# One bank per PSUM pool, the ring of exponentials turned by three places, and layer 1's first channels normalised right behind the last exponential

## The chip, the cores and the metric

The kernel runs on one core of a Trainium2 chip. The core has a matrix engine (TensorE, "PE" in the profile; its weight loads are listed as "PEld"), a vector engine (VectorE, "DVE"), an activation engine (ScalarE, "ACT"), a general engine (GpSimd, "POOL") and a queue engine (SyncE, "SP") that issues most of the transfers. Each engine works through its own queue in order and waits on semaphores for the others. Matmuls write to PSUM, which has eight banks. The metric is the device time of one execution in microseconds (us); a kernel is run several times and the median is compared.

## The reference

Two layers work on x of shape (2, 256, 64, 64): two samples of 256 channels. Cut to what matters:

```python
def _L0_conv_ref(x, qkv_w, qkv_b, num_heads):            # 8 heads of 32 channels, n = 4096 pixels
    ...
    attn_logits = jnp.einsum('bhci,bhcj->bhij', q, k) * scale
    attn_weights = jax.nn.softmax(attn_logits, axis=-1)
    out = jnp.einsum('bhij,bhcj->bhci', attn_weights, v)
...
ctx = _sa(blockify(fq), blockify(fk), blockify(v), oh, ow)   # 64 groups of 64 pixels, stride 8
feats = _bn_relu(_c1x1(ctx, lr_W_w), lr_W_scale, lr_W_shift)
...
ctx2 = _sa(qx, kx, vx, DH, DW)                               # the same on 8 x 8 neighbourhoods
...
return rate1 * out_att + rate2 * out_conv                    # out_conv: a 3 x 3 convolution
...
x = x + _L0_conv_ref(_gn(x), L0_conv_qkv_w, L0_conv_qkv_b, 8)
x = x + _L1_conv_ref(_gn(x), ...)
```

`_gn` is a group normalisation over 8 channels and all pixels. Layer 1 therefore cannot be normalised before layer 0 has ended for those channels.

## The kernel before

Everything runs sample by sample (`b` = 0, 1) through four stages, each with its own PSUM pools, opened and closed in the loop at L1497: `project0` (pool ps0: eight buffers of one bank), `attention0` (pool sc), `layer1_first` (pool ps1: eight buffers), and `layer1_second` (pool pacc with four banks for the convolution, ps2 with four buffers). `bank` takes a buffer of the current pool. A tile of a new pool waits until what lay at its address in the old pool has been read for the last time; with a pool of several banks this holds for the pool's tiles together.

**Channels.** 256 channels are two chunks of 128 (`KC` = 2, k = 0 and 1). The pixels are eight tiles of 512 (`NT`, `T`). A tile of x is `xts[t]`.

**attention0.** A head's 4096 queries are two groups of 2048, so there are 16 groups g per sample. For each group the keys come in 32 blocks j of 128 (`NJ`). A unit is one block by one quarter (512 queries): one score matmul into a bank of `ring` (seven banks of PSUM), and one exponential by ACT (L551) into a place in SBUF. The places form a ring of 28 (`RING`): places 0 to 16 are in the tile `es` (pool apool, tag A), 17 to 27 in `held["es"]`. `at_places` and `runs_of` turn a running count into a place, and split a run of two or three units where the bank ring or one of the two memories ends. `steps` lists the work behind the scores: for each block `add_rows` (DVE adds the exponentials into `added[g]`, L597; for the blocks in `SUMMED` transfers add them in memory, issued by POOL at L605 and L607) and `quarters` (PE multiplies them with the values into `av`, L560; the row sums also go through L560, with `ones`, into a bank of the ring). The loop at L821 interleaves `scores` and `steps`; the queues of PE, ACT and DVE keep the order of the program text (`manual_schedule`).

**The end of attention.** For the last group, blocks 29 to 31 (`SUMMED_LAST`) are not added by DVE: `sum_rows` lets PE sum their rows, with the memory sums `acc` and the DVE sums `added`, in two halves of 256 queries. `steps` emits these row sums behind block 28, then the av products of blocks 29 to 31. `finish_last` then computes the standard deviation of chunk 0 (Sqrt on ACT, L666; reciprocal and shift on DVE), the reciprocals of the row sums (L674), the last context y (in b = 0 copied from PSUM by ACT first, L679), y's statistics, and returns `put`, which writes y into x, and `check`. `Stats.tile` (L321) is a bn_stats per tile of x; those of chunk 1 hang on blocks of the last group.

**layer1_first.** `xg` is the normalised x, regrouped so that each of eight slices of groups takes pixels from all eight tiles t. It has apool's tag A, as `es` has, and apool has one buffer. `to_groups` writes one tile of one chunk of it, on ACT, POOL or DVE (L1171, L1174). Then come, on PE: in b = 0 `fold_products` (weights w3 and fv multiplied with lr and srw, L253 to L280), the mean and variance matmuls of chunk 1 (L328, L337), `firsts` (six projections that need chunk 0 alone), the same with chunk 1 (L1194), and `at_grid` (L1208). After that `group_attention` runs over eight slices. Its last matmuls `pc` go through `to_feats` into `feats`, and `layer1_second` starts from these (`branch`, L1367), with the image copies xp of x on ACT (L1313). In b = 0 DVE also builds the convolution's weights there (`conv_weights`, L857 to L937), whose inputs POOL loads.

**Sample 1's projections.** `following` normalises it while sample 0 ends; `heads4` (L410) projects it.

The lines that set the order at the seam:

```python
if (g, j) == (last, NJ - 3):
    assert len(places) == n_units
    held["rows"] = spare_bank()
    for i in (NJ - 3, NJ - 2, NJ - 1):
        add_rows(g, i)
    sum_rows(g, held["rows"])
```

Of the kernel before, what the change touches and what calls it, by code (L numbers as in the profile page):

```python
# [9 lines left out]
F32 = mybir.dt.float32  # L10
# [30 lines left out]
def direct_layers(ctx: ExitStack, tc: tile.TileContext, a: dict, out: bass.AP, bad: bass.AP):  # L41
# [20 lines left out]
    def bank(shape, name):  # L62
        return psum["ps"].tile(shape, F32, tag="bank", name=name)
# [132 lines left out]
    def fold_scores():  # L196
# [32 lines left out]
        for k in range(KC):  # L229
            block = slice(k * P, (k + 1) * P)  # L230
            pg = bank([P, C + AT], f"pt_g_{k}")
# [17 lines left out]
    def fold_products():  # L249
# [3 lines left out]
        for name, behind in (("w3", "lr"), ("fv", "srw")):  # L253
            turned = w4([P, KC, C], "turned_" + name)
            for j in range(KC):
                pt = bank([P, C], f"pt_{name}_{j}")
                for k in range(KC):
                    nc.tensor.transpose(pt[:, k * P : (k + 1) * P], wts[name][:, k, j * P : (j + 1) * P], ident)
                nc.scalar.copy(turned[:, j, :], pt)
            yield  # L260
            for k in range(KC):
                pt = bank([P, C], f"pm_{name}_{k}")
                for j in range(KC):
                    nc.tensor.matmul(
                        pt, turned[:, j, k * P : (k + 1) * P], outer[behind][:, j, :], start=j == 0, stop=j == KC - 1
                    )
                nc.scalar.copy(wts[name][:, k, :], pt)
            nc.sync.dma_start(out=kept_w[name], in_=wts[name])
            yield
# [138 lines left out]
    def project0(b, xn, w0):  # L408

        def heads4(nm, g):  # L410
            for t in range(NT):
                nt = f"{nm}_{b}_{g}_{t}"
                n = slice(t * T, (t + 1) * T)
                pq = bank([P, T], f"p_{nt}")
# [56 lines left out]
    SUMMED_LAST = (NJ - 3, NJ - 2, NJ - 1)  # L471

    def attention0(b, xts, held):
# [18 lines left out]
        def at_places(first, n):  # L492

            while n > 0:
                at = first % RING
# [7 lines left out]
        recent, spare = [], [0]  # L503
        ring = psum["sc"].tile([P, BANKS, T], F32, tag="ring", name=f"ring_{b}")
# [22 lines left out]
        def runs_of(n):  # L527

            at = n_places
            while n > 0:  # L530
                e = at % RING
# [43 lines left out]
        def add_rows(g, j):  # L575
            if j == 0:
                sums[g] = psum["sc"].tile([P, T], F32, tag="av", name=f"av_{b}_{g}")
# [31 lines left out]
        def work_of(g, j):  # L609


            if (g, j) < (last, NJ - 3):
# [8 lines left out]
        def sum_rows(g, rows):  # L621
            if g == last:
                for part in range(2):
                    for j in SUMMED_LAST:
                        quarters(rows, ones, lambda u: unit(g, j, u), j == SUMMED_LAST[0], False, part)
                    quarters(rows, ones, lambda u: acc[u], False, False, part)
                    quarters(rows, ones, lambda u: added[g][u // 2][:, u % 2, :], False, True, part)
# [31 lines left out]

        def finish_last(g):  # L660
# [5 lines left out]
            nc.scalar.activation(st.rstd[:, first_chunk], st.d[:, first_chunk], AF.Sqrt, bias=eps)  # L666
            rows, avs = held["rows"], copied[g]
            nc.vector.reciprocal(st.rstd[:, first_chunk], st.rstd[:, first_chunk])
            shift = small.tile([P, KC], F32, tag="gn_shift", name=f"shift_{b}")
            st.shift = shift  # L670
            shift_of(st, 0)
            for part in range(2):
                n = slice(part * T // 2, (part + 1) * T // 2)
                nc.vector.reciprocal(avs[:, 1, n], rows[:, n])  # L674
            kept = w4([P, T], f"kept_{b}")
            y = avs[:, 0, :]
            if b == 0:

                nc.scalar.copy(y, sums[g])  # L679
                nc.scalar.copy(kept, rows)  # L680
                nc.vector.tensor_mul(y, y, avs[:, 1, :])
            else:
                nc.scalar.copy(kept, rows)
                nc.vector.tensor_mul(y, sums[g], avs[:, 1, :])
# [69 lines left out]
        for t in range(NT):  # L754
            if t < NT // 2:
                at_block(last, 27 + t, lambda t=t: st.tile(1, t))
            else:
# [16 lines left out]
        def steps():  # L774

            for done in range(NH0 * 2 * NJ):
                g, j = divmod(done, NJ)
                if (g, j) == (last, NJ - 3):
                    assert len(places) == n_units
                    held["rows"] = spare_bank()  # L780
                    for i in (NJ - 3, NJ - 2, NJ - 1):
                        add_rows(g, i)
                    sum_rows(g, held["rows"])
                for _ in work_of(g, j):
# [16 lines left out]
                if j == NJ - 1:  # L801
                    waiting.append(g)
                    avs = w4([P, 2, T], f"avs_{b}_{g}")
                    if g < last:
                        nc.scalar.copy(avs[:, 0, :], sums[g])
                    copied[g] = avs
                    late[:] = [finish(g)]
                    next(late[0])
# [5 lines left out]
        with tc.manual_schedule(engines={E.PE, E.Activation, E.DVE}):  # L814
# [6 lines left out]
            while begun < NH0 * 2 * NJ:  # L821
# [13 lines left out]
                while begun < ready:  # L835
# [7 lines left out]
                    if not final and begun == NH0 * 2 * NJ - 3:  # L843
# [10 lines left out]
            return *finish_last(last), st  # L854
# [194 lines left out]
    def group_attention(nm, q, k, tokens, wv, out, busy=False, apart=False, more=None, split=False, fill=None):  # L1049
# [89 lines left out]
        for m in range(KC):  # L1139
            pc = bank([P, T], f"pc_{nm}_{m}")  # L1140
# [19 lines left out]
    def layer1_first(b, xts, put, check, st):  # L1160


        mean, rstd, shift = st.mean, st.rstd, st.shift

        xg = apool.tile([P, KC, 64, 8, 8], F32, tag="A", name=f"xg_{b}")

        def to_groups(k, t, eng):
            dst = xg[:, k, :, t, :].rearrange("p (d e) o -> p d e o", d=8)
            src = xts[t][:, k, :].rearrange("p (d o e) -> p d e o", d=8, o=8)
            if eng is nc.scalar:  # L1170
                return nc.scalar.activation(  # L1171
# [911 lines left out]
```

## Time and profile before

| | us |
|---|---|
| three runs | 3043.44, 3048.76, 3051.78 |
| median | 3048.76 |
| profiled execution, its own time | 3049.64 |
| its span | 3047.8 |
| attention of sample 0, first to last exponential | 115.13 to 1127.37 |
| attention of sample 1 | 1628.42 to 2643.48 |
| at_grid (L1208) starts | 1159.27 and 2670.63 |
| group attention over slices ends, `branch` starts | 1249.42 and 2756.41 |

Read it so: the "span" is from the first to the last record; what lies around it is 1.8 us. Busy time of PE is modelled, so a busy PE need not be at its peak. A row of a timeline or of a group has the line, the engine, what is written and from what, and in brackets how long the engine was idle before and which instruction ended that. Idle time of an engine costs only where somebody waits for that engine.

### The profile page before, as it was taken

How to read it: one execution, taken by the hardware profiler on the slowest of the kernel's cores; microseconds unless marked ns; L12 is line 12 of the kernel's file. 1: busy time of each engine (PE TensorE's matmuls, PEld its weight loads, DVE VectorE, ACT ScalarE, POOL GpSimd, SP SyncE). 2: the span in 40 equal slices, each digit the busy share in tenths (PEclk: the TensorE clock that was granted, in tenths of full speed). 3: DMA queues.
4: the chain of work that ended last, by engine and by line, in shares of the span. 5: the costliest groups of instructions: out<-in, count | busy, mean ns of one | idle time of the engine just before them, and what ended most of it. 6: DMA issues, size and time to landing. Idle time of an engine off the chain costs nothing. (4 is left out here: it accounts for less than half of the span.)

```text
span 3047.8 us, 63942 instructions
## 1 busy us (share of the span) xinstructions
PE 2972.1 (98%) x25129; PEld 1856.3 (61%) x25129; DVE 2452.3 (80%) x3120; ACT 2341.8 (77%) x3268; POOL 832.3 (27%) x918
## 2 busy tenths in 40 slices
PE   7999999999999999999999999999999999999998
PEld 4556556665556656577765555566555565576765
DVE  4598998989899999856647989989989899835543
ACT  2699999999999984632237999999999999834333
POOL 1022222322223230055401222222222222306440
PEclk9999999999999999999999999999999999999999
DMA  7978789787897761231159688797788976700000
GB/s 260 276 136 181 147 163 174 155 178 150 175 180 157 152 130 37 75 126 42 49 207 270 128 178 161 158 182 146 169 166 166 182 161 130 170 5 4 21 15 23
DMA packets 244420, 425.53 MB, mean 140 GB/s; under 512 B 98904, under 2 KB 109964, under 8 KB 241932
## 3 DMA queue, kind: packets, MB, share of 16 engines
q0 software_dynamic: 94720, 237.57, 40.4%
q1 hardware_dynamic: 149244, 183.51, 21.7%
q8 instruction: 199, 3.26, 0.4%
q14 instruction: 113, 0.93, 0.1%
q10 hardware_dynamic: 144, 0.26, 0.0%
HBM read 120.08 MB, written 68.39 MB: 62 GB/s over the span
## 5 line engine op out<-in xcount | busy, mean ns | idle before, releaser
L551 ACT ACTIVATE es<-ring 128x512 f32<-128x512 f32 (+2 forms) x1572 | 1203.5, 904 | 30.4 <-PE ring L545 22.3
L545 PE MATMUL ring<-q,k 128*128 128x512 f32 x4096 | 1081.8, 407 | 11.6 <-ACT v L551 5.5
L597 DVE TENSOR_TENSOR e<-e,es 128x1024 f32<-128x1024 f32 (+1 forms) x956 | 1035.0, 1143 | 23.3 <-ACT es L551 22.9
L545 PEld LDWEIGHTS ring<-q,k 128*128 128x128 f32 x4096 | 732.3, 188 | 382.5 <-ACT es L551 118.4
L551 ACT ACTIVATE v<-ring 128x512 f32<-128x512 f32 (+2 forms) x1024 | 780.8, 900 | 24.2 <-PE ring L545 12.5
L560 PE MATMUL av<-es,v 128*32 128x256 f32 (+1 forms) x9684 | 724.5, 389 | 0.0
L597 DVE TENSOR_TENSOR e<-e,v 128x1024 f32<-128x1024 f32 (+1 forms) x636 | 669.2, 1107 | 22.6 <-ACT v L551 21.8
L560 PE MATMUL av<-v 128*32 128x256 f32 (+1 forms) x6188 | 497.8, 388 | 0.0
L560 PEld LDWEIGHTS av<-es,v 128*32 128x32 f32 x9684 | 328.0, 109 | 264.6 <-issue 105.0
L560 PEld LDWEIGHTS av<-v 128*32 128x32 f32 x6188 | 221.1, 109 | 170.5 <-issue 72.1
L996 PE MATMUL mm<-v,wf 128*128 128x256 f32 x1024 | 227.6, 380 | 1.5 <-DVE z L1007 1.5
L607 POOL DMA_DIRECT2D es<-es x118 | 100.7, 853 | 463.6 <-ACT es L551 414.0
L996 PEld LDWEIGHTS mm<-v,wf 128*128 128x128 f32 x1024 | 193.3, 190 | 36.8 <-issue 9.8
L986 POOL TENSOR_TENSOR v<-col 128x512 f32<-128x512 f32 x128 | 165.5, 1319 | 178.0 <-ACT rk_sr L1155 39.5
L1003 ACT COPY z<-mm 128x512 f32<-128x512 f32 x32 | 18.7, 586 | 183.3 <-PE mm L996 183.3
L605 POOL DMA_DIRECT2D es<-es x20 | 11.4, 569 | 504.3 <-ACT es L551 445.1
L607 POOL DMA_DIRECT2D acc<-es x118 | 117.9, 1006 | 106.0 <-ACT es L551 40.3
L607 POOL DMA_DIRECT2D es<-v x72 | 61.3, 852 | 290.8 <-ACT v L551 287.4
L1004 DVE TENSOR_TENSOR z<-z,mm 128x512 f32<-128x512 f32 x32 | 22.0, 687 | 126.9 <-ACT z L1003 126.4
L607 POOL DMA_DIRECT2D v<-es x112 | 115.0, 1027 | 18.4 <-ACT es L551 9.0
L607 POOL DMA_DIRECT2D acc<-v x78 | 75.0, 961 | 77.7 <-ACT es L551 27.5
L982 POOL TENSOR_TENSOR col<-xp 128x1152 f32<-128x1152 f32 x32 | 69.6, 2175 | 66.6 <-DVE xp L1448 55.3
(255 smaller groups left out, 2653.0 us busy)
## 6 DMA issues: line engine op xcount, KB each, us to landing
acc<-es POOLq DMA_DIRECT2D x128, 512.0 KB, 6.4
acc<-v POOLq DMA_DIRECT2D x84, 512.0 KB, 6.4
es<-es POOLq DMA_DIRECT2D x138, 256.0 KB, 4.2
v<-es POOLq DMA_DIRECT2D x132, 256.0 KB, 5.0
k<-wk_halves SPq DMA_DIRECT2D x64, 512.0 KB
q<-wq_halves SPq DMA_DIRECT2D x256, 128.0 KB
v<-v POOLq DMA_DIRECT2D x90, 256.0 KB, 4.9
es<-v POOLq DMA_DIRECT2D x84, 256.0 KB, 3.9
```

Of the source, the lines that this page charges most:

```text
L545: touch(nc.tensor.matmul(sc[:, i, :], held["k", g // 2][:, j * P : (j + 1) * P], held["q", g, u // 2][:, u % 2, :], start=True, stop=True, ...
L551: nc.scalar.activation(dst, sc, AF.Exp, scale=SC0), set(range(at % BANKS, at % BANKS + m))
L560: note(nc.tensor.matmul(dst[HD0 * u : HD0 * u + HD0, n], lhs, rhs(u)[:, n], start=start, stop=stop))
L597: nc.vector.tensor_add(dst[:, s, :], dst[:, s, :], src)
L605: nc.gpsimd.dma_start(out=dst, in_=src)
L607: nc.gpsimd.dma_start(out=dst, in_=src, accum_op=ALU.add)
L982: (nc.gpsimd.tensor_add if plus else nc.gpsimd.tensor_sub)(col, cols(one), cols(two))
L986: (nc.gpsimd.tensor_add if plus else nc.gpsimd.tensor_sub)(dst, rows(one), rows(two))
L996: nc.tensor.matmul(mm[:, m, r, :], wf[:, k, 4 * r + q, m * P : (m + 1) * P], v[r // 2][:, r % 2, k, :], start=k == 0, stop=k == KC - 1,)
L1003: nc.scalar.copy(z[:, 1], mm[:, :, 1, :])
L1004: nc.vector.tensor_add(z[:, 0], z[:, 1], mm[:, :, 0, :])
```

## The change

**Banks.** Each stage's general pool becomes pools of one bank each (`open_banks`); `bank` goes round them by a counter, or takes a named one (`at`). The av sums get a pool of their own. The last projection of sample 1 and fold_scores' second product are put in bank 7, the last slice's pc in banks 2 and 3, and ps2 has banks 4 to 7.

**The ring.** Places are turned by three (`RING_SHIFT`). `xg` is no tile of its own but a view of `es` (`Groups`): chunk 0 is places 0 to 7, chunk 1 places 8 to 15.

**The end.** `SUMMED_LAST` has four blocks. Before the row sums, `before_last_rows` emits the Sqrt, two of chunk 1's bn_stats, the standard deviation, and chunk 0's tiles 5 to 7 on POOL and 0 and 1 on ACT; behind them `behind_last_rows` emits the reciprocals and copies by halves (two banks), ACT's tiles 2 to 4 and two more bn_stats. y is always multiplied out of PSUM. ACT's normalise runs through the elements in another order.

**layer1_first.** POOL's order is now also that of the text. `put` comes first; the fold's steps or three projections stand before chunk 1's mean matmul, one more before the variance. Chunk 1 is normalised by half tiles (four of the eight slices at a time). `fold_products` does both transposes first and yields after each product.

The diff, cut:

```diff
+    def open_banks(name, first):
+        stack = ExitStack()
+        places = range(first, 8)
+        psum.update(
+            turn=0, first=first,
+            banks={i: stack.enter_context(tc.tile_pool(name=f"{name}_{i}", bufs=1, space=PSUM)) for i in places},
+        )
+        return stack
+
+    def bank(shape, name, at=None):
+        if at is None:
+            at = psum["first"] + psum["turn"] % len(psum["banks"])
+            psum["turn"] += 1
+        return psum["banks"][at].tile(shape, F32, tag="bank", name=name)
...
+                final = b > 0 and (nm, g, t) == ("wq0", KC - 1, NT - 1)
+                pq = bank([P, T], f"p_{nt}", at=7 if final else None)
...
-    SUMMED_LAST = (NJ - 3, NJ - 2, NJ - 1)
+    SUMMED_LAST = tuple(range(NJ - 4, NJ))
+    N_LAST = len(SUMMED_LAST)
+    N_POOL = 3
+
+    RING_SHIFT = 3
...
-                at = first % RING
+                at = (first + RING_SHIFT) % RING
...
-                sums[g] = psum["sc"].tile([P, T], F32, tag="av", name=f"av_{b}_{g}")
+                sums[g] = psum["av"].tile([P, T], F32, tag="av", name=f"av_{b}_{g}")
...
+        def before_last_rows():
+
+            nc.scalar.activation(st.rstd[:, first_chunk], st.d[:, first_chunk], AF.Sqrt, bias=eps)
+            for t in range(2):
+                st.tile(1, t)
+            nc.vector.reciprocal(st.rstd[:, first_chunk], st.rstd[:, first_chunk])
+            st.shift = small.tile([P, KC], F32, tag="gn_shift", name=f"shift_{b}")
+            shift_of(st, 0)
+            held["groups"] = Groups(es, xts, st)
+            for t in range(NT - N_POOL, NT):
+                held["groups"].normalise(0, t, nc.gpsimd)
+            held["by_act"] = iter(range(NT - N_POOL))
+            by_act(2)
...
+        def behind_last_rows(g):
+
+            avs = copied[g] = w4([P, 2, T], f"avs_{b}_{g}")
+            kept = held["kept"] = w4([P, T], f"kept_{b}")
+            held["y"] = avs[:, 0, :]
+            for part, at in enumerate(held["rows"]):
+                n = slice(part * T // 2, (part + 1) * T // 2)
+                for made in (nc.vector.reciprocal(avs[:, 1, n], ring[:, at, n]), nc.scalar.copy(kept[:, n], ring[:, at, n])):
+                    for other in rows_made[1 - part]:
+                        tc.declare_no_dep(made.ins, other.ins, reason="another bank of the ring")
+                by_act(1 + part)
+            for t in range(2, NT // 2):
+                st.tile(1, t)
...
-                if (g, j) == (last, NJ - 3):
+                if (g, j) == (last, NJ - N_LAST):
                     assert len(places) == n_units
-                    held["rows"] = spare_bank()
-                    for i in (NJ - 3, NJ - 2, NJ - 1):
+                    before_last_rows()
+                    held["rows"] = []
+                    for _ in range(2):
+                        spare_bank()
+                        held["rows"].append(spare[0])
+                    for i in SUMMED_LAST:
                         add_rows(g, i)
                     sum_rows(g, held["rows"])
+                    behind_last_rows(g)
...
-                    if not final and begun == NH0 * 2 * NJ - 3:
+                    if not final and begun == NH0 * 2 * NJ - N_LAST:
                         break
...
+    class Groups:
+
+        def __init__(self, place, xts, st):
+            self.xts, self.st = xts, st
+            self.xg = place[:, 0 : KC * NT, :].rearrange("p a n -> p (a n)").rearrange(
+                "p (k g t o) -> p k g t o", k=KC, g=64, t=8
+            )
+
+        def normalise(self, k, t, eng, half=None):
+            st = self.st
+            first, n = (0, 8) if half is None else (4 * half, 4)
+            order = "p d o e" if eng is nc.scalar else "p d e o"
...
-        with tc.manual_schedule(engines={E.PE, E.Activation, E.DVE}):
+        with tc.manual_schedule(engines={E.PE, E.Activation, E.DVE, E.Pool}):
...
+            for half in range(2):
+                put(nc.gpsimd.tensor_copy, (2 * half, 2 * half + 1))
+            firsts = [lambda t=t, m=m: project(t, m, slice(0, 1)) for t in range(3) for m in range(KC)]
+            for n in range(4 if b == 0 else 3):
+                firsts.pop(0)() if b else next(fold)
+            st.means(second, bank([P, 1], f"pm_l1_{b}"), nc.vector.tensor_copy)
             st.spread(second)
+            firsts.pop(0)() if b else next(fold)
+            st.variances(second, pv := bank([P, 1], f"pv_l1_{b}"))
             st.deviations(second, pv)
             shift_of(st, 1)
...
-            for t in range(NT):
-                done = to_groups(1, t, nc.scalar if t < n_act else nc.vector)
+            for half in range(2):
+                for t in range(NT):
+                    done = groups.normalise(1, t, nc.scalar if t < n_act else nc.vector, half)
...
+                        ends=(2, 3) if t == NT - 1 else None,
```

## The prediction

> **What bounds the kernel now.** I read the engine shares first, then busy time by stretch, then the timeline at each place where one stage hands over to the next, because the title names hand-overs. The profiled execution took 3049.64 us, of which the span is 3047.8.
>
> ```profile
> PE 2972.1 (98%) x25129; PEld 1856.3 (61%) x25129; DVE 2452.3 (80%) x3120; ACT 2341.8 (77%) x3268; POOL 832.3 (27%) x918
> ```
>
> TensorE (PE) is recorded busy for all but 76 us. So a change that takes no matmul away can only win where PE is idle or slow. The chain of waits covers the last 285 us alone (nearly all PE), so I looked for idle PE by stretch. In attention (130 to 1100 us) PE is busy 967.00 of 970.00 and ACT 940.39: two engines near their limit, nothing to win. The second sample's seam between layer 0 and layer 1 looks different (columns: stretch, length, PE, PEld, DVE, ACT, POOL, granted PE clock, DMA):
>
> ```profile
> 2645.00:2650.00 5.00, 4.73 (x88) 2.60 (x80) 4.13 (x7) 0.09 (x1) 0.00 (x0) 1.00 0.08 18
> 2650.00:2655.00 5.00, 1.52 (x20) 0.36 (x8) 4.79 (x6) 4.24 (x5) 4.21 (x2) 0.91 0.58 211
> 2655.00:2660.00 5.00, 1.58 (x4) 1.01 (x5) 2.09 (x9) 2.35 (x2) 4.88 (x4) 0.50 1.02 413
> 2660.00:2665.00 5.00, 5.00 (x10) 2.33 (x9) 3.16 (x7) 3.21 (x4) 1.48 (x3) 0.56 0.76 309
> ```
>
> ACT and POOL have nothing to do from 2645 to 2650; then PE has nothing to do for two stretches, and starts again at half clock. The timeline says who waits for whom (start, duration, in brackets idle before and releaser):
>
> ```profile
> 2641.55 1.93 ACT L551 ACTIVATE v<-ring 128x512 f32<-128x512 f32 x2
> ...
> 2643.53 1.07 PE L560 MATMUL ring<-es,ones 128*32 128x256 f32 x16 [0.16 <-ACT v L551]
> ...
> 2650.79 8.14 POOL L1174 TENSOR_SCALAR xg<-x,mean_l,rstd_l 128x512 f32<-128x512 f32 x3 [11.54 <-PE av L560]
> ...
> 2655.66 0.37 DVE L325 BATCH_NORM_AGGREGATE mv_l<-stats_l 128x2 f32<-128x48 f32 x1
> ...
> 2658.98 2.07 PE L1194 MATMUL py<-xg,wt_g 128*128 128x512 f32 x2 [2.24 <-POOL xg L1174]
> ...
> 2660.84 0.42 PE L337 MATMUL pv_l<-d_l,group 128*128 128x1 f32 x2
> ```
>
> Last exponential at 2643.48; the normalised copy xg takes the exponentials' memory, so POOL starts when PE's last av matmul (to 2651.5) has released it; its third tile ends at 2658.93; the first projection starts there. Twenty py records run until at_grid (L1208) at 2670.63. The first sample is alike: POOL starts at 1134.88 [11.74 <-PE av], projections at 1148.82, at_grid at 1159.27, with weight products between. Three smaller seams each hold a PE wait:
>
> ```profile
> 1543.50 12.71 PE L416 MATMUL p_wk<-xn,wqk 128*128 128x512 f32 x29 [0.87 <-ACT res_sr L1155]
> ```
>
> ```profile
> 1627.89 2.35 PE L545 MATMUL ring<-q,k 128*128 128x512 f32 x9 [1.56 <-DVE hl_wq L422]
> ```
>
> ```profile
> 2756.41 5.40 PE L1367 MATMUL phq_sr<-feats,wt_fq 128*128 128x512 f32 x8 [2.76 <-ACT feats L1155]
> ```
>
> In none is the releaser's data needed by that first matmul: it only empties a bank of the pool before.
>
> **Main seam, second sample.** With the ring turned by three, walking the loop puts the last four blocks (16 units) in places 8 to 23, and blocks 26 and 27 in 0 to 7. So chunk 0 of xg (places 0 to 7) may be written once block 27 is consumed: PE by about 2642.4, DVE's add by 2643.23, the memory adds issued at 2638.07 plus the 6.4 us landing row by 2645.7.
>
> ACT: table load and Sqrt end at 2645.1 as now. DVE then makes rstd and shift at once (0.15 + 0.16), since block 28's two adds (2.33) are gone from its queue: 2645.5. POOL's three tiles follow: 8.14 by the row, to 2653.7. ACT does tiles 0 and 1, a half kept copy, tile 2, the other half, tiles 3 and 4: five at 1.31 less some overlap, plus 2 x 0.35, to 2652.5. Chunk 0 is complete 5.3 earlier than now.
>
> PE: only half a block of av work (0.47) remains behind the last scores, so it waits about 1.1 for the last exponential where it waits 0.16 now. Row sums: eight records take 0.44; six sets (four blocks, acc, added) in two halves make 12 x 0.44 = 5.3, to 2648.8 (now 10 sets, with a wait for DVE's block-28 add inside). Four av blocks of 0.93: to 2652.5, against 2651.5. Queued behind the row sums are av and then everything; this 1.0 is the added cost. The two reciprocals (1.7 each) and two bn_stats end on DVE by 2651.8, so y starts at 2652.6, as now (2652.46), and its chain to the aggregate takes the 3.57 of now: 2656.2.
>
> PE starts projections at 2653.7 after an idle of 1.2. Three at 0.86 (two records of 0.43): 2656.3; the mean matmul; DVE's mean and spread take 1.9 as now: 2658.4; one projection meanwhile; variance to 2658.9; 0.8 to the first chunk-1 normalise. By half tiles the first half takes ACT 3 x 0.7, DVE 5 x 0.43: ready at 2661.9, where full tiles take 3.7. The two other projections end at 2660.6, so PE waits 1.3: **this chain is what is late next.** Eight records of 0.43: at_grid at 2665.4 instead of 2670.6. **-5.2.** Put's copies (2.61 on POOL) end near 2656.7, before their readers.
>
> Here the Trainium skill's page "TensorE: Matmul & The Clock Gate" (Part 1: The HAM clock gate) matters: an idle window of about 3.4 us halves the clock, and as long a busy one restores it. The rows above agree for a 7 us gap (0.50, projections at 0.86 a record). For gaps of 1.0 to 1.3 the nearest row is the first sample's seam, where gaps of up to 2.5 go with clocks of 0.80 to 0.88. By that row 11 us at 0.8 cost 2.2 (gain 3.0), by the rule nothing (gain 5.2). I take the rule: PE is busy for only 59 to 77% of those stretches, and would be for over 80%.
>
> **Main seam, first sample.** The same sums from the last exponential at 1127.37: av ends 1136.5, chunk 0 at 1137.5, transposes and turned copies to 1138.6, w3's products to 1139.7, mean 1140.2, one fv product, variance 1142.5, the rest of the fold (1.9) to 1144.4, six projections (5.2), eight records (3.4): at_grid at 1153.0 instead of 1159.3, **-6.3**. But the convolution-weight work on DVE (L888 onwards, now from 1153.47) starts near 1149.9, only 3.6 earlier: the half tiles cost it 12 x 0.43 against 6 x 0.72. At the stage's end PE already waits behind it (bd, 1.64 and 2.34, DVE held 5.19 for weights). That stall may grow by 0 to 2.7; I take +1.4. **-4.9.**
>
> **Single banks.** Second sample's projections start when pc_sr has ended: -0.9, PE being full behind it. Its scores start as the last projection ends; ACT's own last bias copy ends at 1627.05 and the first exponential now starts at 1628.42: **-1.3**, ACT setting the ramp. In the first sample the exponential waits for its table load anyway (ends 1115.11): 0. At phq, PE gains 1.7, but hq waits for six image copies on ACT up to 2760.48 and runs now at 2761.04: **-0.5**; first sample likewise 0.3. Were ACT ordered otherwise, up to 1.7 and 1.3.
>
> **Turned places.** Splits at a place's or bank's edge: walking the loop gives 1305 exponentials per sample against 1298 (2596 on the page is twice that) and 6 more memory adds. A split costs 2 x 0.65 - 1.09, less 0.09 of overlap, 0.12: 14 make 1.7 if ACT is the limit, 0 if PE is. I take **+0.8**.
>
> **Sum:** -5.2 - 4.9 - 0.9 - 1.3 - 0.8 + 0.8 = -12.3, so 3049.6 - 12.3 = **3037.3**. The median of the runs shown, 3048.76, is 0.9 lower, inside their spread of 8, so I do not shift it.
>
> **Rivals.** (a) *New waits take half back*: clock at 0.8 in the second seam (+2.2), the whole conv-weight stall (+1.3), a pool still released as one because ring is one tile, so the three bank gains fail (+3.0): 3044. For: the rows at 0.80 to 0.88; against: busier seams. (b) *The small ends all fall well*: no stall growth (-1.4), no split cost (-0.8), ACT's image copies behind hq (-2.2): 3033. (c) *Slower*: the split that fell at place 17 (bank 3) now falls at place 0 (bank 4) once each turn of 28 places, 147 turns in all. ACT's waits for ring in attention average 0.34 (14.7 us, 43 times); a new one of 0.2 per turn costs 29: 3067. It decides from 0.09 per turn. Against: the number of edges per turn is unchanged. (d) *It does not do what it says*: were es ordered as a whole, the row sums would wait for POOL's tile at 2653.7, some +10 per sample, 20 in all, against gains of 11.5 there and 2.2 at the three smaller seams after the split cost: 3056. Against: exponentials are written into es all through attention while PE reads it, without such waits.
>
> **Chances.** Forecast 0.60 (3033 to 3041), (a) 0.13, (b) 0.20, (c) 0.05, (d) 0.02. Range 3029 to 3045: (a) and (b) with some 3 us of scatter between medians beside (b). Below about 0.3% (9.1 us) a difference cannot be told from none here: faster needs under 3039.6, which holds for (b), nine tenths of the forecast (0.55) and a little of (a) (0.02): 0.77. Slower needs over 3057.9: (c), 0.05. Same: 0.18.
>
> **What would show it.** Right: POOL's xg starts within 3 us of the last exponential and carries no wait for av; PE's gap before the first py under 2 us at clock 1.0; at_grid about 22 us after the last exponential in the second sample (now 27.1) and 25.6 in the first (now 31.9); p_wk, ring and phq without the waits above. Wrong: row sums waiting for ACT or POOL, py records of 0.86, a longer attention stage, or more PE idle before the first convolution.

## The result and the profile after

| | before | changed |
|---|---|---|
| median of 6 runs, us | 3050.27 | 3027.77 |
| lowest and highest | 3043.44, 3052.64 | 3024.22, 3033.0 |
| profiled execution, its own time | 3049.64 | 3024.22 |
| its span | 3047.8 | 3022.4 |

The ratio is 0.9932, with a 95% interval of 0.9921 to 0.9944: 22.5 us less between the medians, 25.4 between the two profiled spans. The forecast was 3037.3, 12.3 us less. The direction is right, the gain was almost double, and the measured median lies 1.2 us below the low end of the range.

The engine shares of the changed kernel first: PE is recorded busy for 9 us less than before, although it has 32 more records.

```profile
PE 2963.0 (98%) x25161; PEld 1850.1 (61%) x25161; DVE 2443.4 (81%) x3111; ACT 2341.5 (77%) x3288; POOL 843.3 (28%) x930
```

The same work takes PE less time where the granted clock is higher. Before, the profile holds nine half-clock windows of 3.4 us between 15 and 3005 us; after, two. The first sample's twenty projections show it, before (one window at their start) and after (none):

```profile
1148.82 10.52 PE L1194 MATMUL py<-xg,wt_g 128*128 128x512 f32 x20 [1.64 <-ACT xg L1171]
```

```profile
1139.60 8.83 PE L1243 MATMUL py<-es,wt_g 128*128 128x512 f32 x20
```

In the same way w3's eight products take 1.99 us where they took 3.34, and the second sample's py records 2.1 us less. Some 5 of the 12.8 us that the two hand-overs gain are such clock time.

The hand-over of the second sample by stretches of 5 us, from just after its last exponential at 2624.83 (columns: stretch, length, PE, PEld, DVE, ACT, POOL, granted clock, DMA share, GB/s):

```profile
2625.00:2630.00 5.00, 5.00 (x96) 3.02 (x98) 2.20 (x4) 4.29 (x6) 3.18 (x2) 1.00 0.02 5
2630.00:2635.00 5.00, 3.80 (x65) 1.81 (x55) 4.08 (x5) 3.76 (x4) 4.67 (x2) 1.00 0.32 105
2635.00:2640.00 5.00, 4.90 (x14) 2.12 (x15) 3.38 (x12) 0.26 (x1) 2.45 (x4) 1.00 0.93 337
2640.00:2645.00 5.00, 3.81 (x10) 1.50 (x9) 4.97 (x13) 4.72 (x8) 0.00 (x0) 1.00 1.02 417
```

ACT and POOL work at once, PE is busy for 76% of a stretch at the least, and the clock stays at 1.00. The timeline of the changed kernel at the places that the prediction named (start, duration, in brackets idle before and releaser), PE and POOL together:

```profile
2624.89 1.27 PE L582 MATMUL ring<-es,ones 128*32 128x256 f32 x17 [1.02 <-ACT v L573]
...
2626.82 7.85 POOL L1218 TENSOR_SCALAR es<-x,mean_l,rstd_l 128x512 f32<-128x512 f32 x3 [7.23 <-DVE rstd_l L688]
...
2634.92 2.81 PE L1243 MATMUL py<-es,wt_g 128*128 128x512 f32 x6 [1.20 <-POOL es L1218]
...
2642.51 3.67 PE L1243 MATMUL py<-es,wt_g 128*128 128x512 f32 x8 [1.19 <-DVE es L1218]
```

POOL starts 2.0 us after the last exponential and waits for DVE's rstd, no longer for the last output product. The two waits that are left are those the prediction worked out: 1.2 ahead of the first projection, 1.3 ahead of the first of chunk 1.

Where the 25.4 us between the two profiles went, stage by stage:

| stretch | before | after | difference | forecast |
|---|---|---|---|---|
| start to the table load ahead of the first exponential | 113.83 | 112.10 | -1.7 | 0 |
| attention 0, from that load to the last exponential | 1013.55 | 1011.23 | -2.3 | +0.4 |
| hand-over 0: last exponential to at_grid | 31.89 | 25.03 | -6.9 | -6.3 |
| layer-1 slices 0: at_grid to branch | 90.16 | 87.02 | -3.1 | +1.4 |
| branch of sample 0 to first exponential of sample 1 | 378.99 | 372.79 | -6.2 | -2.5 |
| attention 1, first to last exponential | 1015.06 | 1016.66 | +1.6 | +0.4 |
| hand-over 1 | 27.15 | 21.28 | -5.9 | -5.2 |
| layer-1 slices 1 | 85.78 | 84.10 | -1.7 | -0.5, with the next row |
| branch of sample 1 to the end | 291.44 | 292.21 | +0.8 | |

The hand-overs came out within 0.7 us of the forecast. What was not forecast lies elsewhere: attention 0, the slices, and the long stretch between the samples. Not all of these differences belong to the change. The -1.7 at the start is within the scatter: one version of the kernel (image copies on DVE, below) reaches this point at 112.25 us in one profile and at 113.57 in another. And attention 0 of the changed kernel takes 1012.5 us in its second profile (below), 1.1 less than before and not 2.3.

### The profile page after: what moved, and what is told of

Its sections match the earlier page's. It is cut to its first block, busy times and chain, and to the rows that moved or that the text cites. A ratio compares the mean times of both kernels' runs of the same rounds, so it can differ in the third digit from the quotient of the medians.

```text
span 3022.4 us, 64069 instructions
## 1 busy us (share of the span) xinstructions
PE 2963.0 (98%) x25161; PEld 1850.1 (61%) x25161; DVE 2443.4 (81%) x3111; ACT 2341.5 (77%) x3288; POOL 843.3 (28%) x930
## 3 DMA queue, kind: packets, MB, share of 16 engines
q8 instruction: 199, 3.26, 0.5%
## 4 chain that ended last, share of the span: by engine, by line
PE 87%; DVE 5%; DMA 3%; ACT 2%; issue 1%; SPq 0%; ACTq 0%; DVEq 0%; POOLq 0%
PE ring L567 32%; PE av L582 29%; PE mm L1036 7%; PE p_wk L433 2%; PE pv L456 2%; PE p_wq L433 2%; DVE prep L957 2%; PE prq_sr L1417 2%; PE prk_sr L1417 2%; PE pvs_sr L1106 2%; PE phk_sr L1406 1%; PE phq_sr L1406 1%; PE ring L582 1%; PE pvs_lr L1106 1%; PE py L1243 1%
## 5 line engine op out<-in xcount | busy, mean ns | idle before, releaser
L582 PE MATMUL av<-v 128*32 128x256 f32 x6224 | 506.0, 389 | 0.0
L629 POOL DMA_DIRECT2D acc<-es x126 | 129.5, 1033 | 116.4 <-ACT es L573 32.1
L629 POOL DMA_DIRECT2D acc<-v x86 | 87.5, 1017 | 81.9 <-DMA acc<-es 35.5
```

What stands on the lines that cost most here:

```text
L582: note(nc.tensor.matmul(dst[HD0 * u : HD0 * u + HD0, n], lhs, rhs(u)[:, n], start=start, stop=stop))
L629: nc.gpsimd.dma_start(out=dst, in_=src, accum_op=ALU.add)
```

## The experiments

My theory after the result: the hand-over gives 11 to 13 us, single banks 3 to 6, fewer clock windows the rest. Rivals: R1, the banks give much more; R2, the turned ring changes the attention itself; R3, the part not forecast is chance. (The expectations call a sample a batch.)

**Banks alone**, with the named banks and the av sums' own pool (the diff to the kernel before, cut):

```diff
+    def open_banks(name, first):
...
+    def bank(shape, name, at=None):
...
-        with tc.tile_pool(name=f"ps0_{b}", bufs=8, space=PSUM) as psum["ps"]:
+        with open_banks(f"ps0_{b}", 0):
```

> The kernel before with only the single-bank pools, the named banks and the separate pool of the output sums. My theory: they free the first tiles of a stage from waiting for the release of all eight banks of the stage before, and let the bank that is free first be taken; they are worth 3 to 6 us of the 22.5 (3044 to 3047 us, ratio 0.9980 to 0.9990), seen as the missing 0.23-us waits in the second stage and no p_wk and ring waits at the start of batch 1; the stretch from the last exponential to at_grid stays within 1 us of 31.9 and 27.15 us. Rival R1 (the pools carry most of what was not forecast): below 3040 us, ratio below 0.9965. Rival R3 (what was not forecast is chance in the clock and elsewhere): 3049 us or more, ratio 0.9995 or more.

Measured: 3042.71 us (3038.68 to 3046.35), ratio 0.9980 [0.9972, 0.9987]: 6.1 us, at the top of my own bracket. The hand-overs take 30.1 and 27.0 us (31.9 and 27.15 before). The gain sits between the samples, where the stretch from the last convolution of sample 0 to the first exponential of sample 1 falls from 101.53 to 97.24 us. PE's timeline of this run shows how, and it is not what I had forecast:

```profile
1528.48 1.02 PE L429 MATMUL p_wk<-xn,wqk 128*128 128x512 f32 x2
1529.44 1.15 PE L1103 MATMUL sp_sr<-rk_sr,rq_sr 128*64 128x64 f32 x32
1530.52 2.86 PE L1079 MATMUL pvs_sr<-wt_fv,feats 128*128 128x256 f32 x12
1533.21 1.88 PE L429 MATMUL p_wk<-xn,wqk 128*128 128x512 f32 x4
1534.93 0.38 PE L1135 MATMUL at_sr<-ident,e_sr 128*128 128x128 f32 x2
1535.15 1.03 PE L1079 MATMUL pvs_sr<-wt_fv,feats 128*128 128x256 f32 x4
1536.01 1.02 PE L429 MATMUL p_wk<-xn,wqk 128*128 128x512 f32 x2
1536.87 1.95 PE L1155 MATMUL pc_sr<-bd,vs_sr 128*128 128x128 f32 x16
```

Projections of the next sample (p_wk) stand between the small products of the last slice. With a pool of eight banks they could only follow all of it. PE's waits before, 0.45 at sp, 0.17 and 0.87 around pc, 1.56 at the first scores, are all gone. In the same way the next slice's phq now stands between the two parts of pc, where PE waited 0.23 for vs in most slices. The kernel before has the wait, and phq behind it:

```profile
2791.32 0.61 PE L1142 MATMUL pc_sr<-bd,vs_sr 128*128 128x128 f32 x4
2792.16 1.60 PE L1142 MATMUL pc_sr<-bd,vs_sr 128*128 128x128 f32 x12 [0.23 <-ACT vs_sr L1073]
2793.60 1.02 PE L1367 MATMUL phq_sr<-feats,wt_fq 128*128 128x512 f32 x2
```

The changed kernel fills it:

```profile
2767.82 0.61 PE L1182 MATMUL pc_sr<-bd,vs_sr 128*128 128x128 f32 x4
2768.27 1.02 PE L1406 MATMUL phq_sr<-feats,wt_fq 128*128 128x512 f32 x2
2769.13 1.50 PE L1182 MATMUL pc_sr<-bd,vs_sr 128*128 128x128 f32 x12
```

But part of it is given back. In this run ACT waits 2.65 us for a memory add some 29 us into attention 1; the changed kernel has the same wait:

```profile
1632.99 1.70 ACT L573 ACTIVATE es<-ring 128x512 f32<-128x512 f32 x3
1637.25 6.52 ACT L573 ACTIVATE es<-ring 128x1536 f32<-128x1536 f32 x7 [2.56 <-DMA acc<-es]
```

Counted exponential by exponential, the changed kernel's attention 1 falls 2.8 us behind that of the changed kernel with one pool (the next run) within its first 100 exponentials, and stays 2.7 to 3.2 behind to the end. All ten profiles with single banks fall behind there, by 1.7 to 3.5 us against a kernel with one pool. In all fourteen profiles this add is issued 15.4 to 15.9 us after the first exponential and lands 125.5 to 126.5 us after the last convolution. With single banks the attention starts 4.3 us earlier and the issue moves with it, but the landing does not: the add takes 12.4 to 13.4 us instead of 8.5 to 9.2, and most of the earlier start is lost at once. What holds the add until then was not tried.

**The changed kernel with one pool** of eight (or four) banks:

```diff
-            banks={i: stack.enter_context(tc.tile_pool(name=f"{name}_{i}", bufs=1, space=PSUM)) for i in places},
+        psum["ps"] = stack.enter_context(tc.tile_pool(name=name, bufs=8 - first, space=PSUM))
...
-                sums[g] = psum["av"].tile([P, T], F32, tag="av", name=f"av_{b}_{g}")
+                sums[g] = psum["sc"].tile([P, T], F32, tag="av", name=f"av_{b}_{g}")
```

> The changed kernel with one pool of eight (or four) banks per stage again, and the output sums back in the pool of the scores; ring turn, early chunk 0 and half tiles stay. My theory: the layer-1 normalisation writes on-chip memory and not PSUM, so most of the gain stays: 3030 to 3034 us (ratio to before 0.9935 to 0.9950); the first layer-1 matmuls may wait for the last release of the attention, under 2 us a batch. Rival R1: over 3037 us. If chance (R3): 3027 to 3029 us, no difference to the changed kernel.

Measured: 3032.76 us (3028.69 to 3035.08), ratio 0.9950 [0.9937, 0.9964]: 5 us over the changed kernel. The waits at p_wk (0.87), at the first scores (1.56) and the 0.23 in the slices are back, the hand-overs are not longer (25.0 and 21.3). So the banks are worth 5 to 6 us from either side, and need nothing of the hand-over. (5 us is a difference of medians of five and six runs, whose ranges overlap.)

**The turn alone** (kernel before):

```diff
-                at = first % RING
+                at = (first + 3) % RING
...
-                e = at % RING
+                e = (at + 3) % RING
```

> The kernel before with only the places of the exponentials' ring turned by three. It moves addresses, not work: my theory says no difference, 3048 to 3052 us, ratio 0.9990 to 1.0005, attention spans within 1 us of 1013.55 and 1015.06 us. Rival R2 (the turn changes the attention, as the 2.3 us that batch 0's attention became shorter would suggest): 3 us or more off, ratio at most 0.9985.

Measured: 3044.96 us (3035.85 to 3047.98), ratio 0.9984 [0.9978, 0.9991]. My theory falls here: 4.9 us (2.7 to 6.7) from addresses alone. ACT's timeline shows the place; the kernel before, and then the turn alone:

```profile
778.90 0.62 ACT L551 ACTIVATE v<-ring 128x512 f32<-128x512 f32 x1
783.13 4.75 ACT L551 ACTIVATE v<-ring 128x1536 f32<-128x1536 f32 x6 [3.62 <-DMA acc<-v]
```

```profile
777.64 2.04 ACT L551 ACTIVATE v<-ring 128x1024 f32<-128x1024 f32 x3
780.84 3.29 ACT L551 ACTIVATE v<-ring 128x1536 f32<-128x1536 f32 x3 [1.17 <-DMA acc<-v]
```

PE in the kernel before:

```profile
784.64 1.65 PE L545 MATMUL ring<-q,k 128*128 128x512 f32 x5 [2.58 <-ACT v L551]
```

An exponential may not be written into a place that a memory add still reads. Once in each sample ACT waited 3.6 to 3.8 us for such an add; PE, starved, stood still for 2.58 (at 782) and 2.76 us (at 2296). Turned by three, ACT's wait is 1.2, and PE has enough queued to get past it with 0.19. I had looked at PE's total in attention (967.00 of 970.00) and called it "nothing to win"; 2.58 of those 3.0 us were this one wait.

How the 4.9 us divide is not settled. The two attentions are 1.3 and 1.4 us shorter in the profile, less than the time that PE stood still. Seven more exponentials per sample, the splits that the prediction priced, may take the rest; that was not tried. The hand-overs are shorter too (30.0 and 25.9 us), and there are seven half-clock windows instead of nine. One more wait of this kind stands in sample 1: ACT waits 2.15 us at 2419 for a memory add, and PE 1.82. It stays with the turn (2.08) and is gone in the changed kernel, also without the turn; which line removed it was not tried.

**Turned by fourteen instead**, to see whether the time follows that wait:

```diff
-                at = first % RING
+                at = (first + 14) % RING
...
-                e = at % RING
+                e = (at + 14) % RING
```

> The kernel before with the ring turned by fourteen places instead of three. My theory: the turn pays in the attention only through ACT's wait for one memory add (3.6 and 3.8 us without a turn, 1.2 and 1.2 turned by three), so the time follows this wait: if it is near 1 us, 3043 to 3047 us; if it is 3 us or more, 3048 to 3052 us. Rival (the gain of the turn by three is chance or comes from another place): the time does not follow the wait.

Measured: 3053.77 us (3050.6 to 3058.26), ratio 1.0008 [1.0000, 1.0016]: nothing gained, at the edge of a loss. (The hand-over of sample 0 is also 2.3 us longer than before in this profile, 34.2 us, so not all of the difference to the other turn is the wait. And its runs were granted a mean clock of 0.9925 against 0.9935 of the kernel before beside them; if PE is busy throughout, that is up to 3 us, by an estimate of 0.0010 of 3050. For the turn by three it is 0.9946 against 0.9938, up to 2.4 of the 4.9 us.) The wait is there, on another place:

```profile
782.95 6.16 ACT L551 ACTIVATE es<-ring 128x1536 f32<-128x1536 f32 x8 [3.39 <-DMA acc<-es]
```

Over the runs (ACT's longest wait for the add of this stretch in samples 0 and 1, and PE's idle time from 118 to 1120 us, in waits of over 0.15 us):

| | turn | wait | PE idle |
|---|---|---|---|
| before | 0 | 3.6, 3.8 | 3.18 |
| banks alone | 0 | 3.6, 3.4 | 3.14 |
| turn alone | 3 | 1.2, 1.2 | 0.37 |
| turned by fourteen | 14 | 3.4, 3.3 | 3.26 |
| changed, not turned (below) | 0 | 3.8, 3.3 | 3.38 |
| banks and turn (below) | 3 | 1.9, 1.1 | 1.24 |
| changed, one pool (above) | 3 | 1.1, 1.2 | 1.75 |
| changed | 3 | 1.2, 1.2 | 0.18 |

Where the wait is over 3 us, PE is idle for 3.1 to 3.4; where it is under 2, for 0.2 to 1.8. The clock follows the wait in part: the four kernels with the long wait hold eight PE waits of over 2.2 us for it, and a half-clock window begins within 2 us of the end of five of them (in the kernel before, the wait ends at 2298.42 and the window begins at 2299.14). Behind the short wait none begins. Why the add lands some 14.6 us after its issue in the kernel before (768.48 to 783.1) and 10.0 in the turned one (770.83 to 780.8) stays open.

**Banks and turn together**, without the hand-over's code:

> The kernel before with the single-bank pools and the turned ring together, nothing else. If the two gains are of different places and add (6.1 for the pools, 4.9 for the turn, both out of their ratios to the kernel before): 3037 to 3041 us, ratio 0.9955 to 0.9975, and the hand-over itself (early chunk 0, half tiles, four blocks summed at the end, the fold's order) is left with the remaining 9 to 13 us. Rival (the turn only shows where the pools do not, or the other way round): 3042 to 3046 us.

Measured: 3040.6 us (3034.14 to 3044.97), ratio 0.9963 [0.9950, 0.9975]: 11.3 us (7.6 to 15.3), the sum of 6.1 and 4.9 within that interval. With the changed kernel at 0.9932 and 0.9925 (below), 9.5 to 11.6 us are left for the code at the hand-over. In this run the hand-overs take 31.4 and 25.4 us. The runs below take only some of that code apart: four blocks summed at the end, y out of PSUM, ACT's other order and the fold's order were not tried one by one.

**Chunk 0 written at the start of layer 1 again** (in the changed kernel):

```diff
-            for t in range(NT - N_POOL, NT):
-                held["groups"].normalise(0, t, nc.gpsimd)
-            held["by_act"] = iter(range(NT - N_POOL))
-            by_act(2)
...
+            for t in range(5, NT):
+                groups.normalise(0, t, nc.gpsimd)
+            for t in range(5):
+                groups.normalise(0, t, nc.scalar)
```

> The changed kernel, but the normalisation of layer 1's first 128 channels stands at the start of layer 1 again, behind the last multiplication of the attention, with the same eight tiles on POOL and ACT. My theory: this is the main part; the first layer-1 matmul waits again and the stretch from last exponential to at_grid grows by 4 to 6 us per batch, which gives 3036 to 3040 us (ratio 0.9955 to 0.9970). Rival R1 (pools and half tiles carry the gain): within 4 us of the changed kernel, 3027 to 3032 us.

Measured: 3025.93 us (3024.3 to 3029.09), ratio 0.9932 [0.9918, 0.9945], hand-overs 25.0 and 21.3 us: no difference. ACT's timeline tells why:

```profile
2629.42 3.45 ACT L1206 ACTIVATE es<-x,shift,rstd_l 128x512 f32<-128x512 f32 x3 [0.55 <-ACT rstd_l L685]
2632.66 0.42 ACT L700 COPY kept<-ring 128x256 f32<-128x256 f32 x1
```

Three tiles stand ahead of the first copy of row sums, though the text has them behind both copies: from one block of fixed order to the next the compiled order is not that of the text. The run undid the place in the text and not the early start; what it shows is that the hand interleaving brings nothing that can be told in these runs. It needed another edit, one that takes the memory away.

**The same without the turn** (`RING_SHIFT = 0` in that kernel):

> The changed kernel with the ring not turned, so the last exponentials lie in the places that chunk 0 of the normalised copy takes, and with chunk 0's normalisation written at the start of layer 1, as in the run before (whose instruction order came out almost that of the changed kernel). My theory: memory is what lets chunk 0 be early. POOL waits for the last output product again, the stretch from the last exponential to at_grid is 25.5 to 28 us in batch 1 and 29.5 to 32 us in batch 0 (changed: 21.3 and 25.0), and one wait of 3 to 4 us for a memory add comes back on ACT in each attention (some 2.4 us each at the end): 3038 to 3044 us, ratio 0.9960 to 0.9985. Rival (the half tiles, the planner's freedom and the banks carry the hand-over, the turn only the attention): 3031 to 3034 us.

Measured: 3038.97 us (3033.1 to 3040.06), ratio 0.9965 [0.9951, 0.9979]. POOL and then PE wait again:

```profile
2636.57 7.77 POOL L1209 TENSOR_SCALAR es<-x,mean_l,rstd_l 128x512 f32<-128x512 f32 x3 [10.81 <-PE av L582]
```

```profile
2644.40 4.24 PE L1234 MATMUL py<-es,wt_g 128*128 128x512 f32 x6 [5.37 <-POOL es L1209]
```

The hand-over of sample 1 takes 26.7 us instead of 21.3, as expected; that of sample 0 only 26.4 instead of 25.0, where I had expected at least 29.5. There PE has the fold's products to do before the first projection; it waits 2.42 us for w3's turned copy, which stands behind chunk 0's tiles on ACT, and no longer for POOL. So the turn carries 5.4 us of the hand-over in sample 1 and 1.4 in sample 0, and in sample 0 most of the gain belongs to the rest of the code. With the attention, the turn is worth 10 us in the changed kernel by the ratios (0.9965 against 0.9932); the profile of this run is the quickest of its five runs, 5.9 us under their median.

**Full tiles for chunk 1** (in the changed kernel):

```diff
-            for half in range(2):
-                for t in range(NT):
-                    done = groups.normalise(1, t, nc.scalar if t < n_act else nc.vector, half)
+            for t in range(NT):
+                done = groups.normalise(1, t, nc.scalar if t < n_act else nc.vector)
```

> The changed kernel with chunk 1 normalised by full tiles. By the prediction's sum the first chunk-1 projection waits 1.8 us longer in batch 1 and, where convolution weights wait on DVE behind it in batch 0, DVE's queue is 0.8 us shorter: 3027.5 to 3031 us, ratio 0.9930 to 0.9945, and a PE wait of 2.5 to 3.5 us ahead of the first chunk-1 projection of batch 1 (changed: 1.19). Rival (half tiles pay nothing, their extra instructions cost as much as they bring): 3026 to 3028 us with at_grid of batch 1 within 0.5 us of 21.3 after the last exponential.

Measured: 3030.7 us (3027.92 to 3033.32), ratio 0.9937 [0.9924, 0.9951]. The wait ahead of chunk 1 in sample 1 is 2.51 us instead of 1.19, and at_grid follows the last exponential by 22.6 us instead of 21.3; sample 0 is unchanged at 25.0. The half tiles are worth 1.3 us there, against 1.8 worked out; the difference of the medians, 2.9, does not go beyond their scatter.

**Block 28's products first**, to fill PE's 1.02 us wait for the last exponential:

```diff
                 if (g, j) == (last, NJ - N_LAST):
...
                         held["rows"].append(spare[0])
+                if (g, j) == (last, NJ - N_LAST + 1):
                     for i in SUMMED_LAST:
                         add_rows(g, i)
                     sum_rows(g, held["rows"])
```

> The changed kernel, with block 28's output products ahead of the row sums, so that they fill PE's wait of 1.03 us for the last exponential. If PE's own work bounds the hand-over: 0.9 us per batch, 3025.5 to 3027 us. If ACT's normalised tiles and the chain from the last output product bound it, as the wait of 1.20 us ahead of batch 1's first projection says: the wait moves there, batch 1 gains 0 to 0.3 and batch 0, where weight products fill the time, up to 0.9: 3026.5 to 3028 us.

Measured: 3026.8 us (3023.22 to 3031.55), ratio 0.9925 [0.9911, 0.9938]. The wait moves, in the profile of this run:

```profile
2627.80 1.27 PE L582 MATMUL ring<-es,ones 128*32 128x256 f32 x17 [0.16 <-ACT v L573]
...
2637.80 2.81 PE L1244 MATMUL py<-es,wt_g 128*128 128x512 f32 x6 [2.03 <-POOL es L1219]
```

0.86 gained at the row sums, 0.83 lost at the first projection: POOL's three tiles bound the hand-over of sample 1, not PE. The hand-overs are 0.65 and 0.4 us shorter (24.4 and 20.9). In time no difference can be told.

**Image copies on DVE.** After the change PE waits 2.77 us at prq (L1417) in sample 1's first step, as it did at phq before: ACT has image copies ahead of hq.

```profile
2736.68 5.40 PE L1417 MATMUL prq_sr<-hq_sr,wt_fq 128*128 128x512 f32 x8 [2.77 <-ACT hq_sr L1195]
```

In sample 1 seven of them go to DVE: chunk 0 of tiles 0 to 2, whose chunk 1 is there already, and both chunks of tiles 3 and 4:

```diff
-                if both and k == 1:
+                if both:
                     normalise(dst, src, k, mean, rstd)
...
-                    to_image(tt)
+                    to_image(tt, b > 0 and t == 0)
```

> The changed kernel with batch 1's image copies of the first second-stage step (five tiles, both chunks) on DVE instead of half of them on ACT. PE waits 2.77 us at prq for hq, which stands behind those copies in ACT's queue. If that queue is the cause, the wait falls under 1.2 us and the time by 1.5 to 2.5 us (3025 to 3026.5). Rival: hq is late for another reason, or DVE's longer queue makes the first convolution late by as much: 3027 to 3029 us.

Measured: 3021.39 us (3020.29 to 3023.64), ratio 0.9908 [0.9893, 0.9923]. The wait is gone:

```profile
2732.69 1.45 PE L1406 MATMUL phq_sr<-feats,wt_fq 128*128 128x512 f32 x3
2734.15 3.70 PE L1417 MATMUL prq_sr<-hq_sr,wt_fq 128*128 128x512 f32 x8
2737.69 2.54 PE L1036 MATMUL mm<-v,wf 128*128 128x256 f32 x11
```

From branch to the first convolution it takes 7.25 us instead of 11.70: 2.77 are the wait, and 1.70 the eight prq records, which ran under a half-clock window (5.40 us) and now do not (3.70). Against that, PE waits 1.56 instead of 1.11 for DVE and 1.29 instead of 1.01 for ACT just before. That ACT's queue caused this wait is shown. Not all of the 6.4 us below the changed kernel is explained by it: the profile holds no half-clock window between 15 and 3005 us, the changed kernel's two, and the four runs were granted a mean clock of 0.999 against 0.997.

**The changed kernel and the last one again, on one chip:**

> The changed kernel once more, to see which of its differences come back: 3026 to 3030 us, ratio 0.992 to 0.994. If the granted clock's half-speed windows fall by chance, this profile has other ones than 1231.8 and 2737.1 us; the attention of batch 1 (1016.7 us in the first profile, 1015.1 before) shows whether it is longer or scatters.

> The changed kernel with batch 1's first image copies on DVE once more, beside the changed kernel on the same chip. If the missing wait at prq and the clock window behind it are the whole gain: 2.5 to 4.5 us below the changed kernel, 3022.5 to 3025.5 us; if the 6.4 us of the first look stand: 3020 to 3022.5 us; if chance: no difference.

Measured: changed 3028.09 us (3025.79 to 3032.56), ratio 0.9925 [0.9912, 0.9939]; with the image copies on DVE 3025.3 (3024.31 to 3030.76), ratio 0.9917 [0.9904, 0.9931]. That is 2.8 us, in the bracket that the missing wait explains; the 6.4 of the first runs did not come back, and the two intervals overlap. This time both profiles hold three half-clock windows, so the 2.8 us are the better measure of the edit. It has the lowest median of the versions tried, both times. Attention 1 is 1017.2 us in the changed kernel's second profile (1016.7 in the first), longer than before both times, in line with the giving back shown above. The half-clock windows at 1232.9 and 2738.2 us come back within 1.1 us of the first profile's, each behind a PE wait of 2.6 to 2.8 us; one at 116.8 us came new.

## Why the prediction was right, and where its sum was wrong

**The main seam** was right by its steps. Sample 1: chunk 0 free early, POOL at once, PE's first wait 1.2 (forecast 1.2), its second 1.19 (1.3), at_grid 5.9 us earlier (5.2), and the run without the turn takes 5.4 of it away. For the clock I took the Trainium skill's rule ("TensorE: Matmul & The Clock Gate", Part 1: The HAM clock gate) over the neighbouring row at 0.80; the profile shows 1.00 in all four stretches, so the row was not the near one here. That row was also misread: its longest wait is 1.64 us, not 2.5 (2.05 if the wait ahead of the short variance product is added). Sample 0: 6.9 us (6.3), but only 1.4 of it goes when the turn is taken out; the rest of the code brings more than the early chunk there, and 3.0 us are records that no longer run at half clock.

**"That stall may grow by 0 to 2.7; I take +1.4"** did not happen: the slices of sample 0 became 3.1 us shorter. PE's waits at the end of that stretch are 0.45 and 2.74 where they were 1.64, 0.73, 2.34 and 1.33. Every edit tried shortens this stretch: the banks alone by 2.9, the turn alone by 2.1, and the changed kernel with one pool by 3.7. So these gains do not add, none of them was in the sum, and which of them is at work in the changed kernel is not settled. Of the cost that was put on DVE's queue only 0.4 us is seen, in the last wait (2.34 before, 2.74 after).

**"Single banks"** was too small: 3.0 us in the sum, 6.1 measured alone and 5.0 by taking them out. The step that failed is the assumption that only the first matmul of a stage moves ("PE being full behind it"). With single banks matmuls of the next stage fill the waits inside the stage before. The forecast 0.9 at p_wk and 1.3 at the first scores were there, and 2.1 us more around them; against that, 2.8 us were given back in attention 1. What I left open at hq, "were ACT ordered otherwise, up to 1.7 and 1.3", is the wait that the image copies on DVE took away: from at_grid to the end 2.5 and 3.7 us in the two pairs of profiles.

**"Turned places: I take +0.8"** had the wrong sign: 4.9 us gained. I counted splits of exponentials and memory adds, and asked rival (c)'s question, whether a new wait for a bank comes in. The wait that mattered was an old one, for the memory behind a place, and it depends on which place a summed block falls on. The price of the splits itself is not refuted: the attentions gained less than PE's missing idle time. Rival (c)'s loss did not come, yet its point stands in another form: turned by fourteen, the same edit gains nothing.

With these two terms at their measured sizes, and the hand-over left as forecast, the sum is -12.3 - 3.1 - 5.7 = -21.1, against -22.5. That it comes so close is in part luck: the runs with banks or turn alone have shorter hand-overs and slices too, so the three terms overlap.

**The rivals.** (a) named new waits: the clock, the conv-weight stall and the bank gains all went the other way. (b), "the small ends all fall well", had the direction, but of the ends it names only the stall fell well; most of the surplus comes from two mechanisms that it does not name, matmuls that move into earlier waits and the wait for a memory add. (d) is out: POOL starts 2.0 us after the last exponential.

## What to carry over

Before calling a busy engine "nothing to win", list its few longest waits with their releasers: one wait of 2.6 us per sample, and a rotation of addresses that removes it, hid in a 99.7% busy PE. When buffers are split so that they free one by one, price not only the first instruction of the next stage but every wait that its other instructions can now fill, and look for the transfer that does not start earlier with them. And look at the compiled order before trusting an experiment that only moves text: here it moved nothing.

## Unexpected in the hardware

The same PE wait of 2.5 us, at at_sr in the first step of sample 0's second stage, stands in all fourteen profiles of this case. In five of them (before, turn alone, turned by fourteen, full tiles, block 28 first) the clock is halved for one window of 3.4 us right behind it; in nine it is not. The ten microseconds around it, before and then after (columns as above):

```profile
1328.00:1338.00 10.00, 7.28 (x30) 5.79 (x29) 8.56 (x17) 1.48 (x3) 2.15 (x1) 0.83 0.01 2
```

```profile
1316.20:1326.20 10.00, 7.50 (x43) 6.13 (x42) 8.81 (x18) 2.13 (x4) 2.16 (x2) 1.00 0.00 0
```

So a wait shorter than the window can cost the clock or not, and the wait's length does not tell which; perhaps where it falls against the windows does, but no run here shows it. What a window costs can be read from the stretch of convolutions there: 211.4 us with the window (full tiles, block 28 first) against 209.8 to 209.9 without it (the changed kernel and five others with the same code in this stretch), so 1.6 us for one that is filled with work. The nine windows before against two or three after are thus part of the gain, but no separate cause: at most places they vanished with the waits ahead of them.
